# Perceiver block on one core: value matmuls with the weights stationary, and the reciprocal row sums sent through DRAM

## The chip, the cores and the metric

The kernel runs on one core of a Trainium2 chip. The metric is the device time of one execution in microseconds; a run is compared by the median of several executions. The engines of the core are named as in the profile: PE is TensorE's matmul, PEld its weight load, DVE is VectorE, ACT is ScalarE, POOL is GpSimd, and SP issues all DMAs of this kernel, in the order of its queue.

## What is computed

The input is x, 8 sequences of 64 tokens of 512 values, and a context of 1601 rows of 512 values for each sequence. Three sublayers are added to x in turn: an attention block (self attention and cross attention with a common projection), a sparse self attention, and a feed-forward layer with ternary weights. The change touches the cross attention alone. Of the reference:

```python
kvx = jnp.einsum('bsi,oi->bso', cond, w_kv_x)
kx, vx = jnp.split(kvx, 2, axis=-1)
kx = _ln(kx.reshape(b, sc, g, d), kxln_w, kxln_b)
vx = vx.reshape(b, sc, g, d)
xout = _gqa(qx, kx, vx).reshape(b, s, nh * d)
cat = jnp.concatenate([core, xout], axis=-1)
catq = _div_clamp_fp8(cat, proj_smooth)
return jnp.einsum('bsi,oi->bso', catq, wproj) * (proj_in_scale * proj_w_scale)
```

Here cond is the context. There are 8 groups of 2 heads with 128 values each; the softmax runs over the 1601 rows. The result for a head is divided by the sum of its exponentials, rounded to 8 bits with a scale for each value, and projected.

## The kernel before

The cross attention is done in 16 units (`work`, a list of `Cross`): 8 sequences for the first four groups, then 8 for the other four. A unit has 128 query rows for each group (2 heads of 64 tokens), so a tile of 128 partitions by 512 columns holds all four groups side by side, and 13 tiles of context rows (12 of 128, one of 65). One loop over g (L1156) runs the stages of these tiles as a pipeline: `keys` and `keys_t` make the keys of a tile, `scores` the scores of two or three tiles, `exps` the exponentials. `LAG` = 17 steps later `context` loads the context rows again, `probs_t` turns the exponentials, and `weigh` multiplies them with the context rows into four PSUM banks.

Values are not computed for the 1601 rows. Instead the exponentials weigh the raw context (`weigh`, L693 to L695), which gives a 512 x 128 sum for each group, and this sum is multiplied with the value weights afterwards:

- `weighed` (L697), after the unit's last tile, copies the four banks to the SBUF tiles `ut`, and forms `cts`, one over the row sums: a reduce of `csu` (L704) and a reciprocal (L705), 128 x 4.
- `values` (L707), a step later, loads the value weights `wv` in four parts of 256 KB and runs 16 matmuls in fp32 (L714), 4 for each part. `ut` is the stationary operand and `wv` the moving one, so the query row comes out on the partitions and the value's index on the columns. A multiply (L717) from PSUM scales each of the four groups by its column of `cts` and gives `xo`.
- `cat` (L719), one more step later, turns `xo` with four transposes on TensorE (`transpose4`, L219, tile `xt`), since the projection needs the value's index on the partitions. `quant_cat` (L445) scales and rounds the result into `catq`, and `proj_part` (L431) projects it.

Between these steps stands the background work of other stages: projections, self attention, sparse attention and the preparation of the ternary weights are generators that the loop advances by a pace (`PACE`). The order on each engine is not that of the source: the program is recorded with priorities and then placed by a scheduler, which decides the order of each queue and raises work that is ready early.

DMAs that touch the change: `cTr` (L546), the turned context for `keys`; `cr` (L667), the context for `weigh`; `clo`, the low part of the context, which the first half of the units writes to DRAM (L675) and the second half loads (L672). `cTr` and `cr` share a tag of three buffers. POOL makes `cTlo` (L550) from `cTr` after ACT has made `cThi` (L549). A DMA waits in SP's queue for a free buffer, and everything behind it waits too. `xrd` is a DRAM buffer that `proj_part` writes (L437) and reads (L434).

Of the kernel before, what the change touches and what calls it, by code (L numbers as in the profile page):

```python
# [21 lines left out]
P = 128  # L22
# [35 lines left out]
def tile_perceiver(ctx: ExitStack, tc: tile.TileContext, t: dict):  # L58
# [25 lines left out]
    def sm(tag, k=1, dt=F32, bufs=None):  # L84
        kw = {} if bufs is None else {"bufs": bufs}
        return small.tile([P, k], dt, tag=tag, name=nm(tag), **kw)
# [5 lines left out]
    def mainp(tag="m"):  # L92
        return pm.tile([P, 512], F32, tag="m", name=nm(tag))
# [35 lines left out]
    def load(dst, src):  # L129
        nc.sync.dma_start(dst, src)  # L130
        return dst
# [4 lines left out]
    def v3(ap, g):  # L136
        return ap.rearrange("p (g k) -> p g k", g=g)
# [123 lines left out]
    def dtile(shape, dt, tag):  # L261
        return dram.tile(shape, dt, tag=tag, name=tag)
# [8 lines left out]

    wpd = [dtile([P, 2, H], F32, f"wpd{c}") for c in range(32)]
    clod = [dtile([SC, H], F32, f"clod{b}") for b in range(NB)]

    codd = [dtile([3, H], F32, f"codd{b}") for b in range(NB)]
    w1t = dtile([NIC, P, DFF], BF16, "w1t")
# [243 lines left out]
    class Cross:  # L520
# [123 lines left out]
        def last_probs(self):  # L644
# [5 lines left out]
            A.copy(sc[:, :, o + 2], sc[:, :, o])  # L650
            V.tensor_tensor(sc[:, :, o + 1], sc[:, :, o], p1.bitcast(F32), ALU.subtract)

        def context(self, tt):
            t0, n = TT[tt]
            if tt == len(TT) - 1:
                raw = mp.tile([P, 512], F32, tag="raw", name=nm("cr"), bufs=3)
                for h in range(2):
                    load(raw[h * S:(h + 1) * S], t["ctx"][self.b, t0:t0 + S, :])
                chi = mp.tile([P, 512], F32R, tag="chi", name=nm("chi"), bufs=2)
                clo = mp.tile([P, 512], F32R, tag="clot", name=nm("clot"), bufs=1)  # L660
                A.copy(chi, raw)
                V.tensor_tensor(clo[:S], raw[:S], chi[:S].bitcast(F32), ALU.subtract)
                load(clo[S:S + 3].bitcast(F32), codd[self.b])
                self.cc[tt] = chi, clo
                return
            raw = mp.tile([P, 512], F32, tag="raw", name=nm("cr"), bufs=3)
            load(raw[:n], t["ctx"][self.b, t0:t0 + n, :])  # L667
            chi = mp.tile([P, 512], F32R, tag="chi", name=nm("chi"), bufs=2)
            clo = mp.tile([P, 512], F32R, tag="clo", name=nm("clo"), bufs=2)
            A.copy(chi[:n], raw[:n])  # L670
            if self.half:
                load(clo[:n].bitcast(F32), clod[self.b][t0:t0 + n])  # L672
            else:
                V.tensor_tensor(clo[:n], raw[:n], chi[:n].bitcast(F32), ALU.subtract)
                nc.sync.dma_start(clod[self.b][t0:t0 + n], clo[:n].bitcast(F32))  # L675
            self.cc[tt] = chi, clo
# [20 lines left out]
        def weighed(self):  # L697
            self.ut = []
            for ic in range(NIC):
                ut = mp.tile([P, 512], F32, tag="ut", name=nm("ut"), bufs=4)  # L700
                (V.tensor_copy if ic % 2 else A.copy)(ut, self.U[ic])
                self.ut.append(ut)
            ts = self.ts = sm("cts", HG)
            V.tensor_reduce(ts, v3(self.su, HG), AX.X, ALU.add)  # L704
            V.reciprocal(ts, ts)  # L705

        def values(self):  # L707
            po = mainp("xo")
            for ic in range(NIC):
                wv = mp.tile([P, 512], F32, tag="wv", name=nm("wv"), bufs=2)  # L710
                load(wv, t["wkv"][ic * P:(ic + 1) * P, 1024 + self.half * 512:1024 + (self.half + 1) * 512])
                for g in range(HG):
                    s = slice(g * P, (g + 1) * P)
                    PE.matmul(po[:, s], lhsT=self.ut[ic][:, s], rhs=wv[:, s], start=ic == 0 and g == 0, stop=ic == NIC - 1,  # L714
                              skip_group_check=True)
            self.xo = mp.tile([P, 512], F32, tag="ut", name=nm("xo"), bufs=4)
            V.tensor_tensor(v3(self.xo, HG), v3(po, HG), self.ts.unsqueeze(2).to_broadcast([P, HG, D]), ALU.mult)  # L717

        def cat(self, catq):  # L719
            pt = transpose4(self.xo, pt=mainp("xt"))  # L720
            quant_cat(pt, catq, 16 + self.half * 8, self.b % 2, "m1")


    def last_context():
# [431 lines left out]
    for g in range(NA + LAG + 3):  # L1156
        nA, kA = divmod(g, NT)
        if g < NA and kA == 0:
            h = work[nA].half
            if h not in wk:  # L1160
                wk[h] = key_weights(h)
            work[nA].wk = wk[h]
        if g == LAG - 1:
            lane["wide"] = False
        if g == NA + 3:
            lane["late"] = mainp("late")
        e = g - LAG + 1
        if 0 <= e < NA:
            nE, kE = divmod(e, NT)
            w = work[nE]  # L1170
            if kE == CHUNKS[-1][0]:
                w.last_probs()
            w.context(kE)
            w.probs_t(kE)
            ci = CHUNK_OF[kE]
            if ci + 1 < NCH:

                with tc.issue_after(w.pin.ins):
                    w.exps(ci + 1, *((0, 2) if kE == CHUNKS[ci][0] else (2, 4)))
        if g == LAG - 4:  # L1180
            last_context()
        if g < NA:
            work[nA].keys(kA)
        if g == 0:
            bgA.pump(ALL)
        if g == 2:
            bgA.add(norms(rest), projection("qx", range(4), rest), projection("qx", range(4, 8), range(NJ)),
                    projection("q", range(8), range(NJ)), projection("k", range(4), range(NJ)), projection("v", range(4), range(NJ)))
            bgA.add(*[self_attn(j) for j in range(NJ)])
            bgA.add(attn_consts())  # L1190
        if g == TERNARY_AT:
            bgB.add(ternary("ffn_w1", w1t), ternary("ffn_w2", w2t))
        if 0 <= g - 2 < NA:
            nS, kS = divmod(g - 2, NT)
            ci = CHUNK_OF[kS]
            w = work[nS]
            if kS == CHUNKS[ci][-1]:
                if ci == 0:
                    w.queries()
                w.scores(ci)  # L1200
                if ci == NCH - 1:
                    w.maxima()
                    w.exps(0, 0, 2)
        if 0 <= g - 3 < NA and (g - 3) % NT == NT - 1:
            work[(g - 3) // NT].exps(0, 2, 4)
        e = g - LAG
        if 1 <= e and e % NT == 0 and e // NT <= len(work):
            work[e // NT - 1].values()
        if 2 <= e and (e - 1) % NT == 0 and (e - 1) // NT <= len(work):
            w = work[(e - 1) // NT - 1]  # L1210
            key = (w.b // 2, w.half)
            j, odd = divmod(w.b, 2)
            split = w.half and j >= NJ - SPLIT
            if not odd:
                bgA.clear_front()
                if w.half:
                    bgA.pump(ALL)
                catq[key] = cat_tile("catx")
            w.cat(catq[key])
            if key != (NJ - 1, 1):  # L1220
                if not w.half:
                    if odd:
                        bgA.front.append(proj_part(j, 16, catq[key]))
                elif split or odd:
                    on = (odd * S, S) if split else (0, P)
                    bgA.add(finish(j, 24, catq[key], *on))
            elif not odd:
                bgC.add(proj_weights(24), finish(NJ - 1, 24, catq[key], 0, S, True, Late()))
            else:
                bgA.add(finish(NJ - 1, 24, catq[key], S, S, True))  # L1230
        if 0 <= e < NA:
            nE, kE = divmod(e, NT)
            work[nE].weigh(kE)
            if kE == NT - 1:
                work[nE].weighed()
        if 0 <= g - 1 < NA:
            nT, kT = divmod(g - 1, NT)
            work[nT].keys_t(kT)
        for bg, q in ((bgA, PACE[g >= LATER]), (bgC, PACE[1]), (bgB, TERNARY_PACE if g < NA + FFN_AT else 0)):
            n = int((g + 1) * q) - int(g * q)  # L1240

            with tc.issue_after(pin[0].ins), tc.issue_after(paced[0].ins) if bg is bgB else nullcontext(), tc.high_priority( -100):
                bg.pump(n)
        if g == NA + FFN_AT:
            bgB.pump(ALL)
            if NJ > 2:
                bgB.add(ffn(list(range(NJ - 2)), 0))
                bgB.step()
# [74 lines left out]
```

## Time and profile before

| | |
|---|---|
| median of 3 runs | 1990.03 us (1985.24 to 1996.01) |
| the profiled execution | 1991.72 us, its span 1990.0 us |
| granted TensorE clock, mean | 0.991 |
| PE busy | 1923.4 us |
| DVE, ACT, POOL busy | 1377.2, 1215.9, 634.1 us |
| DMA | 296,503 packets, 352.02 MB, 55.5% of 16 engines' span |
| packets under 512 B | 30,336 |

Busy time is the union of an engine's instructions, so overlapping matmuls are not counted twice, while the mean of one is its full length. In a row of the groups, the first number after the bar is the union in us, the second the mean in ns; after the second bar stand the idle time just before these instructions and what ended most of it. In a timeline a row gives the start and the length in us. The windows give, for each stretch, its length and then the busy time of PE, PEld, DVE, ACT and POOL, each with a count, the granted clock, the DMA share and GB/s.

The wait of SP's own queue is told apart by what it waited for:

```profile
SPq L546 <- POOL cTlo L550: 329.8, 141, 9.9
SPq L130 <- PE acc L695: 181.8, 79, 7.6
SPq L675 <- DVE clo L674: 122.6, 58, 8.6
```

The columns are the total in us, how often, and the longest. SP mostly waits for buffers to come free: loads are issued as early as the buffers allow.

### The profile page before, as it was taken

What the parts mean: (1) busy time and instruction counts of PE and PEld (TensorE: products, weight loads), DVE (VectorE), ACT (ScalarE), POOL (GpSimd) and SP (SyncE); (2) the same over time, 40 slices, a digit from 0 to 9 for tenths busy, and PEclk for the clock granted to TensorE, in tenths of its full rate; (3) what the DMA queues carried; (4) which work ended last, traced back from release to release, by engine and by line L of the source; (5) the groups of instructions that cost most, each with busy time, mean ns of one, the idle gap of its engine ahead of it and who ended that gap; (6) DMA issues with size and microseconds to landing.
All of it is one profiled execution on the core that took longest, in us unless ns stands there. A gap on an engine that the chain in (4) does not pass through costs nothing.

```text
span 1990.0 us, 32306 instructions
## 1 busy us (share of the span) xinstructions
PE 1923.4 (97%) x10709; PEld 1593.6 (80%) x10709; DVE 1377.2 (69%) x3423; ACT 1215.9 (61%) x2724; POOL 634.1 (32%) x600
## 2 busy tenths in 40 slices
PE   7899999999999999999999999999999999999998
PEld 5678888888888887887888788888877787886776
DVE  7768688677678676776775665756577665655665
ACT  6576667666676566655664545555675566566554
POOL 6343334333333333223332323222233333220132
PEclk9899999999999999999999999999999999999999
DMA  6345545466455654557776667656745543564425
GB/s 199 115 140 164 160 143 162 142 209 211 132 171 157 216 160 122 186 172 265 236 265 225 200 199 257 200 188 204 269 136 162 172 157 94 156 209 139 142 65 178
DMA packets 296503, 352.02 MB, mean 177 GB/s; under 512 B 30336, under 2 KB 191232, under 8 KB 296336
## 3 DMA queue, kind: packets, MB, share of 16 engines
q1 hardware_dynamic: 296336, 349.97, 55.5%
q8 instruction: 84, 1.38, 0.3%
q14 instruction: 83, 0.68, 0.1%
HBM read 283.94 MB, written 65.68 MB: 176 GB/s over the span
## 4 chain that ended last, share of the span: by engine, by line
PE 83%; DMA 7%; DVE 5%; issue 2%; ACT 1%; POOL 1%; SPq 0%; POOLq 0%; ACTq 0%; DVEq 0%
PE kx L555 26%; PE acc L693 8%; PE acc L694 8%; PE acc L695 8%; PE s L598 6%; PE pj L340 4%; PE pt L630 4%; PE kx L219 4%; DMA ws<-wpd 3%; PE xo L714 3%; PE pp L431 2%; PE p L822 1%; DMA wv<-in_wkv 1%; PE tr L372 1%; PE y L1073 1%
## 5 line engine op out<-in xcount | busy, mean ns | idle before, releaser
L550 POOL TENSOR_TENSOR cTlo<-cTr,cThi 128x512 fp32r<-128x512 f32 (+1 forms) x208 | 274.4, 1320 | 891.2 <-PE kx L555 618.1
L694 PE MATMUL acc<-plo,chi 128*128 128x512 f32 x768 | 310.3, 405 | 0.4 <-DVE plo L641 0.4
L695 PE MATMUL acc<-phi,clo 128*128 128x512 f32 x768 | 303.8, 397 | 0.0
L562 DVE TENSOR_REDUCE kxv<-ksq 128x4 f32<-128x516 f32 (+1 forms) x208 | 142.9, 687 | 223.0 <-ACT ksq L560 222.8
L173 POOL TENSOR_TENSOR rqk<-kxv,mhalf 128x4 f32<-128x4 f32 (+1 forms) x208 | 217.8, 1047 | 127.1 <-DVE kxv L562 109.5
L693 PE MATMUL acc<-phi,chi 128*128 128x512 f32 x768 | 246.7, 402 | 1.7 <-ACT chi L670 1.0
L555 PE MATMUL kx<-wkhi,cThi 128*128 128x512 f32 (+1 forms) x832 | 240.8, 411 | 7.0 <-ACT wkhi L501 2.3
L549 ACT CAST cThi<-cTr 128x512 fp32r<-128x512 f32 (+1 forms) x208 | 125.9, 606 | 182.1 <-PE kx L555 84.1
L555 PE MATMUL kx<-wklo,cThi 128*128 128x512 f32 (+1 forms) x832 | 230.4, 397 | 0.0
L555 PE MATMUL kx<-wkhi,cTlo 128*128 128x512 f32 (+1 forms) x832 | 229.4, 395 | 0.0
L577 ACT ACTIVATE kthi<-kx,cols 128x512 fp32r<-128x512 f32 (+1 forms) x208 | 140.8, 677 | 137.2 <-PE kx L219 135.6
L670 ACT CAST chi<-cr 128x512 fp32r<-128x512 f32 x192 | 119.1, 620 | 141.7 <-PE acc L694 130.5
L618 ACT ACTIVATE S<-S,cnm 128x256 f32<-128x256 f32 (+1 forms) x384 | 197.1, 522 | 7.0 <-DVE cnm L613 6.8
L578 DVE SCALAR_TENSOR_TENSOR ktlo<-kx,cols,kthi 128x512 fp32r<-128x512 f32 (+1 forms) x208 | 150.9, 726 | 60.7 <-ACT kthi L577 59.9
L555 PEld LDWEIGHTS kx<-wklo,cThi 128*128 128x128 f32 (+1 forms) x832 | 155.0, 187 | 41.2 <-issue 1.6
L555 PEld LDWEIGHTS kx<-wkhi,cTlo 128*128 128x128 f32 (+1 forms) x832 | 154.3, 186 | 41.3 <-issue 3.2
L555 PEld LDWEIGHTS kx<-wkhi,cThi 128*128 128x128 f32 (+1 forms) x832 | 147.5, 188 | 39.2 <-ACT wkhi L501 3.5
L564 DVE TENSOR_TENSOR kn<-kn,rqk 128x512 f32<-128x512 f32 (+1 forms) x208 | 149.4, 718 | 39.4 <-POOL rqk L173 36.3
L602 DVE CUSTOM_DVE_ANT_0 S<-s,zeros 128x256 f32<-128x256 f32 (+1 forms) x384 | 151.9, 429 | 33.1 <-PE s L598 32.2
L694 PEld LDWEIGHTS acc<-plo,chi 128*128 128x128 f32 x768 | 145.0, 189 | 26.4 <-issue 1.7
L693 PEld LDWEIGHTS acc<-phi,chi 128*128 128x128 f32 x768 | 139.9, 189 | 32.7 <-ACT chi L670 2.8
L695 PEld LDWEIGHTS acc<-phi,clo 128*128 128x128 f32 x768 | 144.6, 189 | 26.1 <-issue 1.6
(344 smaller groups left out, 3770.5 us busy)
## 6 DMA issues: line engine op xcount, KB each, us to landing
cTr<-in_ctxT SPq DMA_DIRECT2D x192, 256.0 KB
cr<-in_ctx SPq DMA_DIRECT2D x192, 256.0 KB
ws<-wpd SPq DMA_DIRECT2D x88, 512.0 KB
clod<-clo SPq DMA_DIRECT2D x96, 256.0 KB
clo<-clod SPq DMA_DIRECT2D x96, 256.0 KB
wv<-in_wkv SPq DMA_DIRECT2D x64, 256.0 KB
tern<-in_ffn_w SPq DMA_DIRECT2D x64, 256.0 KB
wpd<-ws SPq DMA_DIRECT2D x32, 512.0 KB
```

Of the source, the lines that this page charges most:

```text
L173: GP.tensor_tensor(y[:n], v, mhalf[:n, :k], ALU.pow)
L550: GP.tensor_tensor(clo[:, :, :n], raw[:, :, :n], chi[:, :, :n].bitcast(F32), ALU.subtract)
L555: PE.matmul(ps[:n], lhsT=st[:, ic, :n], rhs=mv[:, ic, :], start=k == 0, stop=k == 11)
L562: V.tensor_reduce(v[:n], sq[:n], AX.X, ALU.add)
L564: pin[0] = V.tensor_tensor(v3(kn[:n], HG), v3(kn[:n], HG), r.unsqueeze(2).to_broadcast([n, HG, D]), ALU.mult)
L577: A.activation(hi[:, :, o], v3(pt, HG)[:, :, :n], AF.Copy, scale=hw["kx"])
L578: V.scalar_tensor_tensor(lo[:, :, o], v3(pt, HG)[:, :, :n], hw["kx"], hi[:, :, o].bitcast(F32), ALU.mult, ALU.subtract)
L602: V.tensor_tensor_reduce(sc[:, g, :cw], ps[:, :cw], zeros.to_broadcast([P, cw]), 1.0, -3.0e38, ALU.add, ALU.max, self.mx[:, g * NCH + ci:g ...
L618: A.activation(self.S[ci][:, g, :cw], self.S[ci][:, g, :cw], AF.Exp, bias=self.nmx[:, g:g + 1], accum_out=self.su[:, g * NCH + ci:g * NCH ...
L693: PE.matmul(self.U[ic], lhsT=chi[:n, s], rhs=phi[:n], start=tt == 0, stop=False)
L694: PE.matmul(self.U[ic], lhsT=chi[:n, s], rhs=plo[:n], start=False, stop=False)
L695: PE.matmul(self.U[ic], lhsT=clo[:n, s], rhs=phi[:n], start=False, stop=False)
```

## The change

The operands of the value matmuls are exchanged: `wv` is stationary and `ut` moves. The product comes out turned, with the value's index on the partitions and the query rows on the columns, as the projection needs it, and the four transposes of each unit are left out. The factor one over the row sum then belongs to a column and no longer to a partition. A new method `sums` reduces and inverts as before, writes the 128 x 4 factors to DRAM in turned order (512 single words), and loads them back as a row of 512 that is spread to all 128 partitions (`tsr`, one buffer). The multiply takes this tile as its second operand. `sums` is called after `probs_t` of the unit's last tile, one step before `weighed`, where the reduce and reciprocal stood.

```diff
+    tsd = [dtile([HG, P], F32, f"tsd{i}") for i in range(2 * NB)]
...
+        def sums(self):
+
+            ts = sm("cts", HG)
+            V.tensor_reduce(ts, v3(self.su, HG), AX.X, ALU.add)
+            V.reciprocal(ts, ts)
+            d = tsd[self.half * NB + self.b]
+            with nc.allow_non_contiguous_dma(reason="512 words"):
+                nc.sync.dma_start(d.rearrange("g p -> p g"), ts)
+            self.ts = load(mp.tile([P, 512], F32, tag="tsr", name=nm("tsr"), bufs=1),
+                           d.rearrange("g p -> (g p)").partition_broadcast(P))
...
-            ts = self.ts = sm("cts", HG)
-            V.tensor_reduce(ts, v3(self.su, HG), AX.X, ALU.add)
-            V.reciprocal(ts, ts)
...
-                    PE.matmul(po[:, s], lhsT=self.ut[ic][:, s], rhs=wv[:, s], start=ic == 0 and g == 0, stop=ic == NIC - 1,
+                    PE.matmul(po[:, s], lhsT=wv[:, s], rhs=self.ut[ic][:, s], start=ic == 0 and g == 0, stop=ic == NIC - 1,
...
-            V.tensor_tensor(v3(self.xo, HG), v3(po, HG), self.ts.unsqueeze(2).to_broadcast([P, HG, D]), ALU.mult)
+            V.tensor_tensor(self.xo, po, self.ts, ALU.mult)
...
-            pt = transpose4(self.xo, pt=mainp("xt"))
-            quant_cat(pt, catq, 16 + self.half * 8, self.b % 2, "m1")
+            quant_cat(self.xo, catq, 16 + self.half * 8, self.b % 2, "m1")
...
+            if kE == NT - 1:
+                w.sums()
```

## Prediction

> **What bounds the kernel now.** I read the page's busy shares first, then its chain of waits, to see whose time makes the span.
>
> ```profile
> PE 1923.4 (97%) x10709; PEld 1593.6 (80%) x10709; DVE 1377.2 (69%) x3423; ACT 1215.9 (61%) x2724; POOL 634.1 (32%) x600
> ...
> PE 83%; DMA 7%; DVE 5%; issue 2%; ACT 1%; POOL 1%; SPq 0%; POOLq 0%; ACTq 0%; DVEq 0%
> ```
>
> TensorE is busy 97% of the span and is 83% of the chain that ended last; no other engine is above 69%. The granted clock row is 9 in all slices but one. So a change pays by what it takes off TensorE's queue, and costs by what makes TensorE wait. Next, the groups by line with shapes kept apart, for the touched instructions (name, count | total busy us, mean ns | idle before them).
>
> ```profile
> L714 PE MATMUL xo<-wv,ut 128*128 128x128 f32 x512 | 67.1, 280 | 2.6 <-DMA wv<-in_wkv 2.5
> L219 PE MATMUL xt<-ident,xo 128*128 128x128 f32 x64 | 9.8, 275 | 0.1
> L717 DVE TENSOR_TENSOR xo<-xo,cts 128x512 f32<-128x512 f32 x16 | 11.0, 690 | 14.6 <-PE xo L714 14.6
> L445 DVE TENSOR_TENSOR m1y<-xt,rsm 128x512 bf16<-128x512 f32 x16 | 11.0, 686 | 7.4 <-PE xt L219 7.4
> ```
>
> The only TensorE work that goes is the 64 transposes of L219, before which TensorE idled 0.1 us in all: they cost their own length, no wait.
>
> **Removed: 64 transposes.** Their length is not 275 ns each, as they overlap. The timeline of TensorE at the third of the 16 places (start, length):
>
> ```profile
> 472.58 0.40 PE L695 MATMUL acc<-phi,clo 128*128 128x512 f32 x1
> 472.82 0.60 PE L219 MATMUL xt<-ident,xo 128*128 128x128 f32 x4
> 473.26 0.60 PE L219 MATMUL kx<-ident,kn 128*128 128x128 f32 x4
> ```
>
> Four transposes hold the queue from 472.82 to 473.26, 0.44 us. The same distance, from each transpose's start to the next TensorE start, summed over all 64 in the trace, is **6.6 us** (103 ns each). Here a rule disagrees: the Trainium skill, "TensorE: Matmul & The Clock Gate", Part 4 (PE-mode transpose), gives about 275 ns for a 128x128 transpose inside a kernel. That is the row's mean of one, 275, but read as a cost it would save 64 x 0.275 = 17.6 us and put the kernel at 1974; the starts in this trace say 6.6. Between them lies the row's union, 9.8 us. I take 6.6 as TensorE is fed back to back; 9.8 is the end kept for the range. All of it is on the path.
>
> **Operands swapped in L714.** 512 weight loads and 512 matmuls of 128x128 before and after: the same row, cost 0. The first of a group needs both operands in either form. The weight load already waits for the wv load today.
>
> **The multiply and the quantization.** L717 keeps its shape and its 690 ns, with a full row operand instead of a broadcast column. L445 reads SBUF instead of PSUM; the nearest row, the same operation from SBUF (L306, b1y<-ld), has a median of 683 against 692: 16 x 0.01 us, nothing; by its mean of 803 it would be 1.9 us on VectorE, which is 69% busy and is not the end. What goes is VectorE's wait on xt, 7.4 us, and 16 tiles fewer in the three-bank PSUM pool; late next is the multiply's own wait for the matmuls (14.6), which stays. In the last unit the multiply ends at 1876.63 and m1y starts at 1878.50 because the transposes stand at 1877.79: 1.9 us of a dependent chain that goes. But in the built order of the changed program 64 feed-forward matmuls (fh) instead of 32 stand ahead of the last projection, some 32 x 0.114 us = 3.7 us, partly in holes where TensorE now waits for wv (1.4 us at 1871.08). I count the end at -1 us, bounds -3 and +3.
>
> **The sums moved.** Reduce and reciprocal are 174 and 172 ns, 16 of each, before and after. In the source they move up a step, but the scheduler had already raised them: in both built orders they stand right behind the same neighbours (plo, L641). Cost 0.
>
> **Added: 32 DMAs on SP and a wait.** Per unit one store of 512 single words and one load that spreads 2 KB to 128 partitions (256 KB). Sixteen loads are 4.2 MB on 352, with the 16 DMA engines 55.5% used: under 1 point. Issue: a 64-word load took 0.5 us on SP, a cTr load with 512 pieces 0.38; so 0.4 to 0.6 us each, some 16 us of SP over the run. The wait is what matters: SP works in order, and the load stands until the store has landed. Behind it stand the next cTr, cr, clo or weight loads, and for those TensorE waits. The timeline of the first unit:
>
> ```profile
> 193.02 0.18 DVE L705 RECIPROCAL cts<-cts 128x4 f32<-128x4 f32 x1
> ```
> ```profile
> 191.75 1.17 SPq L130 DMA_DIRECT2D cr<-in_ctx  x2
> 194.89 0.39 SPq L546 DMA_DIRECT2D cTr<-in_ctxT  x1
> ```
>
> The reciprocal ends at 193.2 and SP is free. The multiply L717 of this unit starts at 242.5: the row has 49 us to arrive, and in the 16 units 25 to 67 us. The consumer's side is hidden whatever the store takes here. On SP, the nearest wait in this trace is a store to DRAM that is read straight back, xrd:
>
> ```profile
> SPq L130 <- DMA xrd<-xr: 32.2, 13, 5.8
> ```
> ```profile
> 453.45 0.34 SPq L437 DMA_DIRECT2D xrd<-xr  x1
> 457.99 0.34 SPq L130 DMA_DIRECT2D xr<-xrd  x1
> ```
> ```profile
> 455.00:460.00 5.00, 5.00 (x37) 4.65 (x36) 3.58 (x7) 3.23 (x8) 2.44 (x2) 1.00 0.45 137
> 460.00:465.00 5.00, 4.97 (x33) 4.21 (x32) 2.86 (x12) 2.77 (x7) 1.32 (x2) 1.00 0.88 280
> ```
>
> Thirteen such waits, 2.5 us on average, 5.8 the longest. One of 4.2 us (453.8 to 458.0) is followed by ten microseconds in which TensorE (second number) is busy 5.00 and 4.97 of 5: SP's stall reached nobody. With 0.5 us for the store's issue, 2.5 to land and 0.4 for the load, SP is held 3.4 us from the reciprocal. Today its next issue comes 0.4 to 4.5 us after it, 2.2 on average over the units, so what follows is 1.2 us later on average and 3.0 at most. Its cover: the cTr load behind each reciprocal is used by TensorE 15 to 21 us after its issue in 13 of 14 units (it could be there in about 5: 2.9 at the shortest from load to cast, 0.6 cast, 1.3 split; in the fourteenth it is issued 6.5 us after the reciprocal and isn't moved), and the clo load 5.4 to 12.8 us. Cost **0**; if the cover is gone, each microsecond beyond it is 16 us.
>
> The store itself is the unknown. A rule speaks against it: the Trainium skill, "DMA: Bandwidth & Descriptors", Rules for kernel authors, says a last dimension that isn't contiguous makes one descriptor per element and should be rearranged; its Specifications add that pieces under 512 B are read, modified and written. The page gives 0.2 us for an access to memory, 2 at high load (Latency and other measured facts). Were the 32 words per DMA engine done one after the other at 0.2 us, an estimate from that page, the store would take 6.4 + 2.5 = 9 us, 10 us of SP with the issues. By the row a cTr load of as many pieces arrives within 2.9 us, pieces overlapping. I take the row, and keep 10 us as the far end; the near end is nothing.
>
> **Sum.** 1991.7 (the profiled execution; span 1990.0) - 6.6 - 1 = 1984. The median of the runs shown is 1.7 us lower than the profiled one, so **1983 us**, 0.35% faster. A difference under 0.5% (1980 to 2000) is about what a measurement of this kernel can't tell from no change.
>
> **Rivals.** *More than the transposes goes* (1976): the union of 9.8 instead of 6.6, TensorE's wait for wv of 2.6 and the whole 1.9 of the last chain. For it: the new order fills the wv holes at the end; against: TensorE takes these holes elsewhere when its queue shifts. 1991.7 - 9.8 - 2.6 - 1.9 - 1.7 = 1976.
>
> *SP becomes the wait* (slower): one place, the load behind the scattered store. It decides where SP's hold exceeds today's 2.2 us plus the cover: some 10 us for cTr, 3 to 10 for clo in the second half of the units, say 8; so from 10 us. At 12 us, 2 x 16 = 32 us come on: 1983 + 32 = 2015. For it: the rule; against: the xrd row and the depth of the prefetch.
>
> *The gain is dealt away* (1992): the scheduler places all instructions anew, and a quarter of TensorE's built order stands differently. Summing each TensorE start's distance to the next beyond what is usual for its shape (227 ns for L555, whose mean is 240) gives some 165 us of small stalls today; 5% more of them is 8 us and eats the gain: 1983 + 9 = 1992. Nothing in the profile speaks for either sign.
>
> **Numbers.** Forecast 0.42 (its own range 1978 to 1989: 0.12 under 1980, 0.30 within), more 0.22 (faster), SP 0.13 (0.10 slower, 0.03 within), dealt away 0.23 (0.15 within, 0.08 slower). So faster 0.34, same 0.48, slower 0.18. The range, 1973 to 2003, takes in the 1974 of the rule's 275 ns and the dealt-away case with twice its stalls, and leaves out most of the SP case.
>
> **What would show it.** No xt rows, and TensorE's count down by 64, its busy time by 7 to 10 us. SP's wait for tsd at 16 times 2 to 3 us. No wait of VectorE on tsr. If I am wrong, TensorE or POOL waits for cTr, clo or cr behind each tsr load, or the stalls between TensorE starts grow away from these places.

## The result, and the profile after

The changed kernel takes 2115.65 us (median of 6 runs, 2107.97 to 2118.91) against 1987.67 us before: a ratio of 1.0616 (95% interval 1.0593 to 1.0639). It is 6% slower. The ratio is formed from the single runs and not from these two medians, whose quotient is 1.064. Its profiled execution took 2118.8 us with a span of 2117.1 us, 127.1 us more than before. From its page, the busy shares, the granted clock by slice and the DMA packets:

```profile
PE 1959.5 (93%) x10645; PEld 1613.2 (76%) x10645; DVE 1377.7 (65%) x3423; ACT 1210.6 (57%) x2724; POOL 630.0 (30%) x600
...
PEclk9999999999999998999999999999999999999999
...
DMA packets 307256, 356.25 MB, mean 168 GB/s; under 512 B 39041, under 2 KB 199937, under 8 KB 307089
```

TensorE has 64 matmuls fewer, as foretold, and 36 us more of busy time. The 127 us can be told from this line alone: TensorE's idle time is the span less its busy time, 157.6 us against 66.6, so the change adds 91 us of idle time and 36 us of busy time, although 64 transposes are gone: other matmuls took longer. The clock by tenths hides why they took longer (a slice of 53 us is too coarse), but its mean doesn't: 0.964 granted over the span against 0.991. VectorE, ScalarE and POOL are busy for as long as before. 8,705 packets under 512 B were added: 512 words in each of 16 units, and about 16 packets more for each of the 32 added DMAs.

Next, what SP's queue and the engines waited for (total us, times, longest). The first line of the second block is from the kernel before, the others are from the changed one:

```profile
SPq L130 <- DMA tsd<-cts: 129.4, 16, 9.9
```
```profile
ACT cThi L549 <- DMA cTr<-in_ctxT: 32.0, 24, 3.8
ACT cThi L550 <- DMA cTr<-in_ctxT: 149.0, 36, 11.0
...
PE kx L556 <- ACT kn L562: 33.3, 10, 5.8
```

SP stood 8.1 us on average in each of 16 units until the scattered store had landed, that is, until all its words were written; I had put 2.5. ScalarE's wait for the `cTr` load went from 32.0 us to 149.0. VectorE never waits for `tsr`.

The first unit shows the whole chain. SP's timeline:

```profile
192.37 0.39 SPq L661 DMA_DIRECT2D tsd<-cts  x1
200.01 0.33 SPq L130 DMA_DIRECT2D tsr<-tsd  x1
200.43 0.39 SPq L547 DMA_DIRECT2D cTr<-in_ctxT  x1
```

Windows of 2 us behind the store (length; busy PE, PEld, DVE, ACT, POOL, each with a count; clock, DMA share, GB/s):

```profile
192.00:194.00 2.00, 2.00 (x17) 1.86 (x16) 1.16 (x4) 1.69 (x5) 1.28 (x1) 1.00 0.67 140
194.00:196.00 2.00, 2.00 (x17) 1.87 (x16) 0.92 (x5) 1.27 (x3) 1.01 (x2) 1.00 0.00 0
...
200.00:202.00 2.00, 2.00 (x13) 1.57 (x12) 0.00 (x0) 0.00 (x0) 0.00 (x0) 1.00 0.00 0
202.00:204.00 2.00, 2.00 (x12) 1.71 (x11) 0.00 (x0) 0.00 (x0) 0.00 (x0) 1.00 0.45 97
204.00:206.00 2.00, 0.40 (x2) 0.00 (x0) 0.00 (x0) 0.00 (x0) 0.00 (x0) 1.00 0.88 192
...
210.00:212.00 2.00, 2.00 (x6) 1.52 (x6) 1.73 (x5) 1.40 (x5) 0.90 (x1) 0.50 0.80 261
```

Read the columns from right to left as time goes on: the DMAs move nothing, then ScalarE, VectorE and POOL have nothing to do, then TensorE runs out, and when it starts again its clock is 0.50. The timelines of ScalarE and of TensorE tie the ends together:

```profile
207.00 0.62 ACT L550 CAST cThi<-cTr 128x512 fp32r<-128x512 f32 x1 [9.51 <-DMA cTr<-in_ctxT]
...
208.01 0.58 ACT L562 COPY kn<-kx 128x512 f32<-128x512 f32 x1
```
```profile
204.01 0.39 PE L707 MATMUL acc<-phi,clo 128*128 128x512 f32 x1
208.64 1.73 PE L556 MATMUL kx<-wkhi,cThi 128*128 128x512 f32 x4 [4.24 <-ACT kn L562]
210.17 1.91 PE L556 MATMUL kx<-wklo,cThi 128*128 128x512 f32 x4
```

The cast of the late `cTr` tile stands at the head of ScalarE's queue for 9.5 us. TensorE doesn't need that tile yet; it waits for `kn`, a copy of an earlier tile out of PSUM, which stands behind the cast. After 4.2 us without work four matmuls take 1.73 and 1.91 us; four of these usually take 1.17 and 1.08.

### The profile page after: what moved, and what is told of

Read it like the earlier page. It is cut to its first block, busy times and chain, and to the rows that moved or that the text cites. A ratio compares the mean times of both kernels' runs of the same rounds, so it can differ in the third digit from the quotient of the medians.

```text
span 2117.1 us, 32261 instructions
## 1 busy us (share of the span) xinstructions
PE 1959.5 (93%) x10645; PEld 1613.2 (76%) x10645; DVE 1377.7 (65%) x3423; ACT 1210.6 (57%) x2724; POOL 630.0 (30%) x600
## 5 line engine op out<-in xcount | busy, mean ns | idle before, releaser
L556 PE MATMUL kx<-wkhi,cThi 128*128 128x512 f32 (+1 forms) x832 | 253.1, 427 | 41.7 <-ACT kn L562 33.3
L550 ACT CAST cThi<-cTr 128x512 fp32r<-128x512 f32 (+1 forms) x208 | 125.9, 606 | 282.9 <-DMA cTr<-in_ctxT 149.0
L556 PE MATMUL kx<-wklo,cThi 128*128 128x512 f32 (+1 forms) x832 | 239.8, 410 | 0.0
L556 PEld LDWEIGHTS kx<-wkhi,cThi 128*128 128x128 f32 (+1 forms) x832 | 152.7, 196 | 79.0 <-ACT kn L562 37.4
L556 PEld LDWEIGHTS kx<-wklo,cThi 128*128 128x128 f32 (+1 forms) x832 | 162.9, 196 | 43.4 <-issue 0.8
```

Of the source, the lines that this page charges most:

```text
L556: PE.matmul(ps[:n], lhsT=st[:, ic, :n], rhs=mv[:, ic, :], start=k == 0, stop=k == 11)
```

## The experiments

Two theories for the loss: the store of single words clogs the DMA engines, so that loads behind it land late (A), or SP is held behind the load that waits for it, and what is queued there starts late (B). A third was that the swapped operands or the new order of the queues cost by themselves (C). The runs in one table; the ratio is to the kernel before on the same chip, and the last column the ratio as time. For the change this is 122 us, and 128 by its two medians.

| run | median us | ratio (95% interval) | us |
|---|---|---|---|
| the change | 2115.65 | 1.0616 (1.0593 to 1.0639) | +122 |
| no store, no load | 1987.69 | 0.9977 (0.9963 to 0.9990) | -5 |
| scattered store alone | 2092.43 | 1.0491 (1.0460 to 1.0521) | +98 |
| pieces of 16 bytes | 2007.04 | 1.0074 (1.0048 to 1.0099) | +15 |
| turned on TensorE, stored whole | 1993.72 | 1.0003 (0.9989 to 1.0016) | +1 |
| scattered read | 1983.37 | 0.9968 (0.9946 to 0.9989) | -6 |
| hold without scatter | 2000.27 | 1.0038 (1.0020 to 1.0055) | +8 |
| words stored into SBUF | 1987.07 | 0.9974 (0.9957 to 0.9992) | -5 |
| words 512 bytes apart | 1988.98 | 0.9986 (0.9971 to 1.0002) | -3 |
| words 64 bytes apart | 1986.85 | 0.9982 (0.9965 to 0.9998) | -4 |
| turned, issued by POOL | 2001.05 | 1.0058 (1.0039 to 1.0076) | +12 |

### No store and no load

```diff
...
-                nc.sync.dma_start(d.rearrange("g p -> p g"), ts)
-            self.ts = load(mp.tile([P, 512], F32, tag="tsr", ...
+            self.ts = tsr1
```

> The changed kernel with store and load left out: the multiply takes a constant row of ones, so the division by the row sums is missing from the output. The swapped operands and the missing transposes stay. Theory A (the store of 512 single words clogs the DMA engines, and loads behind it land late) and theory B (SP is held behind the load that waits for the store) both expect 1983 us, 6.6 us under before, with the clock back at 0.99. Theory C (the swap or the new order of the queues costs by itself) expects over 2080 us.

0.9977: the swap and the missing transposes are together a small gain, and theory C is out. Here `tsr1` is the constant row.

### The scattered store alone

```diff
-            self.ts = load(mp.tile([P, 512], F32, tag="tsr", ...
+            self.ts = tsr1
```

> The changed kernel with the scattered store of 512 words kept and the load left out (the multiply takes a constant row of ones, so the division is missing from the output): SP waits for nothing. Theory A expects most of the loss to stay, 2060 to 2115 us, with cTr loads that land late behind each store. Theory B expects it to go: 1985 us.

1.0491. Four fifths of the loss stay with nobody waiting for the store: 5.1 of the 6.4% between the change and the kernel without store and load. The first unit again, SP's timeline and windows of 2 us:

```profile
192.38 0.39 SPq L663 DMA_DIRECT2D tsd<-cts  x1
194.04 0.38 SPq L549 DMA_DIRECT2D cTr<-in_ctxT  x1
```
```profile
194.00:196.00 2.00, 2.00 (x17) 1.87 (x16) 0.91 (x5) 1.26 (x3) 1.02 (x2) 1.00 0.15 12
196.00:198.00 2.00, 2.00 (x11) 1.61 (x10) 2.00 (x8) 1.49 (x4) 0.00 (x0) 1.00 0.23 3
198.00:200.00 2.00, 2.00 (x10) 1.69 (x9) 1.81 (x5) 0.00 (x0) 0.00 (x0) 1.00 0.48 40
200.00:202.00 2.00, 2.00 (x13) 1.55 (x12) 0.00 (x0) 0.00 (x0) 0.00 (x0) 1.00 0.43 18
```

Now `cTr` is issued 1.7 us behind the store and not 8, and still 3 to 40 GB/s move and ScalarE runs dry at the same place. In the trace, ScalarE's cast of that tile starts 11.0 us after the load's issue, on average over the units; in the kernel before it starts 4.5 us after it. Theory A holds for the larger part.

### Pieces of 16 bytes

```diff
-    tsd = [dtile([HG, P], F32, f"tsd{i}") for i in range(2 * NB)]
+    tsd = [dtile([P, HG], F32, f"tsd{i}") for i in range(2 * NB)]
...
-                nc.sync.dma_start(d.rearrange("g p -> p g"), ts)
+            nc.sync.dma_start(d, ts)
...
-            V.tensor_tensor(self.xo, po, self.ts, ALU.mult)
+            V.tensor_tensor(v3(self.xo, HG), v3(po, HG), self.ts.rearrange("p (k g) -> p g k", g=HG), ALU.mult)
```

> The factors are stored as they lie, 128 pieces of 16 bytes instead of 512 of 4, loaded in that order, and the multiply reads the row with a stride. Theory A: a quarter of the pieces clogs for a quarter of the time; the store lands after 3 to 4 us instead of 8, and the kernel takes about 2000 us. Theory B: SP is still held for 3 to 4 us, about half of 8, so about 2040 us if the loss goes with the hold.

1.0074. The load is issued 2.7 us after the store on average, not 9.1. Against the kernel without store and load the loss falls to about a sixth, further than the number of pieces. Part of what is left isn't the store: with the stride the multiply takes 1,059 ns instead of 690, and the hold and the spread load are still there.

### Turned on TensorE and stored whole

```diff
-                nc.sync.dma_start(d.rearrange("g p -> p g"), ts)
+            pt = mainp("tst")
+            PE.transpose(pt[:HG, :P], ts, ident)
+            tt = mp.tile([P, P], F32, tag="tst", name=nm("tst"), bufs=1)
+            V.tensor_copy(tt[:HG], pt[:HG, :P])
+            nc.sync.dma_start(d, tt[:HG])
```

> The factors are turned by one transpose on TensorE (4 columns used), copied to SBUF and stored as 4 contiguous pieces of 512 bytes; the load is unchanged. Theory A: nothing clogs; 1985 to 1990 us. Theory B: SP is still held 2.5 to 3 us for each of 16 units, which at the loss per microsecond of the changed kernel (128 us for 129 us held) is about 2030 us.

1.0003: the whole change, with a turned store, equals the kernel before. It has a transpose and a copy of its own, and SP waits 23.1 us in all for the stores; which of these gives the gain of 0.2% back wasn't parted. The store also comes later here, in the first unit at 213.4 us instead of 192.4.

### A scattered read

```diff
-                nc.sync.dma_start(d.rearrange("g p -> p g"), ts)
+                nc.sync.dma_start(ts, t["bout"].rearrange("(g p) -> p g", g=HG))
...
```

> Neither store nor spread load: in their place one load of 512 single words from DRAM into the 128 x 4 tile, in the turned order of the store (the factors are overwritten and a constant row is multiplied, so the division is missing from the output). If 512 pieces of 4 bytes clog the DMA engines by their number (A1), this takes about 2090 us, like the store alone. If it is small writes to DRAM that clog (A2), 1988 us, like the kernel with neither.

0.9968: 512 single words read from DRAM cost nothing that shows. It isn't the number of pieces.

### The hold without the scatter

Against the kernel with the turned store:

```diff
             nc.sync.dma_start(d, tt[:HG])
+            tu = load(mp.tile([P, P], F32, tag="tsu", name=nm("tsu"), bufs=1)[:HG], d)
+            d = tse[self.half * NB + self.b]
+            nc.sync.dma_start(d, tu)
```

> The turned, contiguous store, but with two round trips through DRAM one after the other (4 pieces of 512 bytes each time) before the row is spread: SP stands for three waits in each unit, 6 to 8 us in all, as long as behind the scattered store, and nothing clogs. Theory A: 1990 to 2000 us. Theory B (SP's hold is what costs): about 2090 us. If the hold has the share by which store and load took longer than the store alone (2116 against 2092), 2010 to 2020 us.

1.0038. SP's own waits (total us, times, longest):

```profile
SPq L130 <- DMA tsd<-tst: 23.2, 13, 4.0
SPq L668 <- DMA tsu<-tsd: 16.3, 14, 2.8
SPq L130 <- DMA tse<-tsu: 15.7, 15, 2.1
```

They add to 55 us, 3.4 for each unit against the 8.1 of the change; from the first store to the spread load pass 6.7 us on average, against 9.1. That costs 0.6% over the kernel without DRAM, 12 us, a tenth of the loss. So a hold isn't free, as I had said it would be. But the run doesn't settle what the change's own hold costs: it is shorter here, and it lies 23 us later in the first unit (the first store is issued at 215.3 us), at another place in SP's queue. The difference of the change to the store alone, 1.25% or 25 us, is the hold behind a clogged queue and the spread load together; these two weren't parted.

### Words stored into SBUF

```diff
...
-                nc.sync.dma_start(d.rearrange("g p -> p g"), ts)
+                nc.sync.dma_start(row[:, 0:8:2].unsqueeze(2), ts.unsqueeze(2))
...
```

> The same 512 single words are stored into another SBUF tile, four words of each partition with gaps between them, instead of DRAM; no load (a constant row is multiplied, so the division is missing from the output). A1 (the number of pieces): about 2090 us. A2 (small writes to DRAM): 1988 us.

0.9974: 512 single words written to SBUF cost nothing that shows. They stand less close there than in DRAM, since each partition holds only four of them.

### Words 512 and 64 bytes apart

```diff
-    tsd = [dtile([HG, P], F32, f"tsd{i}") for i in range(2 * NB)]
+    tsd = [dtile([HG, P, P], F32, f"tsd{i}") for i in range(2 * NB)]
...
-                nc.sync.dma_start(d.rearrange("g p -> p g"), ts)
+                nc.sync.dma_start(d.rearrange("g p k -> p g k")[:, :, 0:1], ts.unsqueeze(2))
...
```

> The scattered store alone, but each word goes to a DRAM address of its own 512 bytes from the next, instead of next to one another within 2 KB; no load (a constant row is multiplied, so the division is missing from the output). If neighbouring words clog because their writes meet in the same stretch of DRAM (A3), about 1990 us. If each small write costs by itself, 2090 us as with the store alone.

0.9986. The windows of the first unit, whose store was issued at 190.41, with 512 bytes between the words:

```profile
192.00:194.00 2.00, 2.00 (x17) 1.87 (x16) 0.88 (x5) 1.23 (x3) 1.05 (x2) 1.00 0.35 89
194.00:196.00 2.00, 2.00 (x10) 1.63 (x9) 2.00 (x9) 1.52 (x4) 0.00 (x0) 1.00 0.14 42
196.00:198.00 2.00, 2.00 (x10) 1.67 (x9) 1.85 (x5) 0.62 (x1) 0.00 (x0) 1.00 0.23 72
198.00:200.00 2.00, 2.00 (x13) 1.55 (x13) 1.03 (x2) 1.97 (x4) 1.87 (x2) 1.00 0.56 191
```

The same 512 packets, and the loads flow again. With 16 words in place of the last 128 (64 bytes apart):

> The scattered store alone, each word 64 bytes from the next (next to one another cost about 105 us, 512 bytes apart nothing; no load, a constant row is multiplied, so the division is missing from the output). If the writes meet within 64 bytes of DRAM, this takes about 1988 us; if within a longer stretch, such as 512 bytes, up to 8 words still meet instead of 128: between 2000 and 2092 us.

0.9982, like the kernel without any store. So it is neither single words as such nor writes to DRAM as such that clog, but words less than 64 bytes apart. One load shows it most plainly: in the first unit of all three kernels `cTr` is issued 1.7 us behind the store. The last of its 512 packets starts 11.2 us after the issue behind words next to one another, and 2.4 and 2.3 us after it behind words 512 and 64 bytes apart. GB/s that arrived in each microsecond from the store's issue, mean over the 16 units (before: from the end of the reciprocal), summed from the traces' packets:

```
us from the issue         0   1   2   3   4   5   6   7   8   9  10  11
before                  193 134  89 161 200 171 213 256 191 148 153 167
the change              133 102  88  48  27  21  14  14  15  16  52 124
scattered store alone   163  90  77  41  29  28  35  38  27  28  32 121
pieces of 16 bytes      143 105  91  89 167 197 234 247 268 243 192 148
words 64 bytes apart    148  84  99 145 178 193 169 241 197 185 183 169
```

Behind the store alone 27 to 41 GB/s arrive in the columns 3 to 10, about a fifth of the 173 that the row of before has on average, although SP isn't held. In the change it is 14 to 52, but there SP also stands. Open is where the writes meet, how close below 64 bytes single words have to be, and whether loads of another queue would have been held too: all loads of this kernel go through SP's.

### Turned, issued by POOL

Against the kernel with the turned store:

```diff
-            nc.sync.dma_start(d, tt[:HG])
+            GP.dma_start(d, tt[:HG])
...
+            GP.dma_start(self.ts, d.rearrange("g p -> (g p)").partition_broadcast(P))
```

> A version meant to be the best whole one: the turned, contiguous store and the spread load, both issued by POOL instead of SP, so that SP is never held. If the 6 us by which the turned store on SP lies above the kernel without DRAM (1994 against 1988) are SP's hold, about 1988 us. If POOL's own queue, where the waiting load stands ahead of cTlo and rqk, takes its place: 1995 to 2010 us.

1.0058, so slower than on SP. POOL's waits name the load (total us, times, longest):

```profile
POOL tsr L666 <- DMA tsd<-tst: 11.0, 5, 7.2
```

SP's wait has gone to POOL, where `cTlo` and `rqk` stand behind it. The waits name this place; that it is what costs the time wasn't tried. No version here beats the kernel before as a whole: those that are faster leave the division out.

## Why the prediction was wrong

*The transposes, 6.6 us.* Right in size: the five kernels with the swap and without clogging, hold or spread load stand at 0.9968 to 0.9986, 3 to 6 us under before; 6.6 of 1990 is 0.33%, inside the intervals of four of them (0.10 to 0.37% for the kernel without store and load). The 17.6 us of 275 ns for each transpose, which is the length of one and not its cost (0.88%), are outside all of these intervals: the largest gain any of them allows is 0.54%, 11 us. The further 1 us at the end can't be seen. Two roundings in the sums are off, 1984 less 1.7 is 1982 and not 1983, and 5% of the small stalls adds 8 us and not 9; neither matters.

*Swap, sums, multiply, quantization at nothing.* Right, as far as the kernel with neither store nor load can tell.

*The store lands in 2.5 us.* This is the step that failed: "By the row a cTr load of as many pieces arrives within 2.9 us, pieces overlapping. I take the row". The row was of a read, and of pieces with 512 bytes each, and the 2.5 us were of `xrd`, a store of whole rows. The words do leave the queue quickly, with 7 to 9 ns for nearly every one in the packets' records, but next to one another in DRAM they took 8 us to land, for which I had kept only the far end of my estimate: 9 us from store to load. Measured are 9.1 on average, 7.6 to 11.1. That this number was close is luck, since its reason doesn't hold: words 64 bytes apart are as many accesses, and free. The rule of the Trainium skill that pieces under 512 B are read, modified and written ("DMA: Bandwidth & Descriptors", Specifications) may stand behind this, but no run shows a cost at that bound: a word with 64 bytes to itself, far below it, cost nothing that shows.

*SP's hold is all that the store can cost.* This was the second fault: I asked only who stands behind the waiting load on SP, and gave the store itself no effect on other loads. But it also held loads that wait for nothing and were issued behind it. That is 102 of the 127 us by which the change lies over the kernel without DRAM. The rival, *SP becomes the wait*, named the right place and the wrong mechanism, and had no loss at 9 us.

*The cover of 15 to 21 us.* It was measured to the wrong consumer. TensorE uses the tile that late, but in the trace of before ScalarE's cast of it starts 3.3 to 5.8 us after the issue, and in five of the 14 units the load is already what the cast waits for. Copies that TensorE needs at once stand behind the cast in ScalarE's queue. The trace shows this in the first unit (9.51 and 4.24 us above), and by the list of waits in ten places, 33.3 us; no run takes the cast out of the way, so its share wasn't tried. Nor is it the only path. TensorE stops behind 15 of the 16 stores, 78 us in all; 31 of them end with that copy, and three stops, 18 us, with a load of the projection's weights. The wait for these before and after:

```profile
PE pp L431 <- DMA ws<-wpd: 8.7, 7, 2.2
PE pp L432 <- DMA ws<-wpd: 25.6, 8, 7.7
```

I had named weight loads as standing behind the store, and worked out no cover for them.

*No term for the clock.* The stops behind the stores last 2.8 to 7.7 us. In the 4 us after each of 3.3 us or more the granted clock is 0.50 to 0.61 on average; after the shortest it is 1.00. Mean clock times span is missing 76.2 us of full speed after and 17.9 before: 58 us more, which fits 36 us of longer busy time plus the 10 us that the transposes no longer take, and some idle time at the lower clock. The page "TensorE: Matmul & The Clock Gate" of the Trainium skill (Part 1) says that after an idle window of about 3.4 us the clock is halved until a busy one. The trace agrees in part: its stretches at half clock last 3.4, 6.8 or 10.2 us, the last one apart, but in the kernel before a stop of 2.2 us (at 906.2) was followed by 0.60, so these runs show no sharp bound. Here 91 us of idle time came with 46 us of slower matmuls: a stall cost about half as much again, and I had priced it one to one.

## What to carry to other kernels

A transposing store of single words next to one another isn't a small DMA: it can all but stop the loads behind it for some 8 us, and that reaches every prefetch at once. Turn the few words on an engine first, or keep them 64 bytes apart (tried here for the store alone). And measure the slack of a load to the first engine that waits for it in its queue, not to the engine that is the bound.

## What the runs showed of the hardware

- Behind 512 words of 4 bytes stored side by side into 2 KB of DRAM, the loads of the same queue moved 27 to 41 GB/s for about 8 us, instead of some 170. The same words 64 or 512 bytes apart, read instead of written, or written to SBUF, left no loss to be seen. With pieces of 16 bytes side by side, the load that waits for the store was issued 2.7 us behind it on average, instead of 9.1.
- The packets' own records don't tell: 7 to 9 ns for nearly every 4-byte packet in all cases. It shows in the landing, in the packets behind, and in GB/s.
- After 4.2 us without a matmul four matmuls of 512 columns took 1.91 us instead of 1.08, at a granted clock of 0.50.
